# A gated feed-forward stage on one Trainium2 core: one low-rank input in the place of a redundant row, the other added by VectorE

## The chip, the cores and the metric

The kernel runs on one core of a Trainium2 chip. Its engines run side by side, each through its own list of instructions in order: TensorE (PE; PEld is its loading of weights), VectorE (DVE), ScalarE (ACT), GpSimd (POOL) and SyncE (SP), which here does nothing but issue DMAs. A DMA issue that has to wait for data holds up every issue behind it in the same list. Matmul results land in eight banks of PSUM; a bank is free again when the engines that read it are done. The time is the device time of one execution in microseconds (us), the median of several runs.

## The reference

x is 8 x 256 tokens of 512 features. Everything starts from the layer norm xn of x. An attention branch (128 heads with a low-rank latent and rotary parts) gives s, a feed-forward branch gives g, and the result is x + s * silu(g). The change concerns the feed-forward branch only:

```python
def _layernorm(x, axis=-1, eps=1e-05):
    m = jnp.mean(x, axis=axis, keepdims=True)
    v = jnp.var(x, axis=axis, keepdims=True)
    return (x - m) / jnp.sqrt(v + eps)
...
def _qlora_linear(x, wq, A, B):
    w = jnp.tile(wq, (1, 4))
    base = x @ w.T
    lora = x @ A.T @ B.T
    return base + lora * LORA_SCALING
gate = jax.nn.silu(_qlora_linear(x, w1q, a1, b1))
up = _qlora_linear(x, w3q, a3, b3)
return _qlora_linear(gate * up, w2q, a2, b2)
```

Each weight is one quarter (1376 x 128 for w1q and w3q) repeated four times, so the product with the 512 features is a product of the 128 x 1376 quarter with the sum of the four quarters of xn. On top of it comes a term of rank 2. Since xn has mean zero, its 512 features sum to zero, and so do the 128 rows of the quarter sums: any one of these rows is minus the sum of the others.

## The kernel before

The tokens are taken in four blocks (tb = 0 to 3) of 512. `first_phase` (L304) does the feed-forward stage for all four, and in block 3 also slips in the first pieces of the attention stage; it fills about the first 238 us. After it comes a long loop over heads and batches, which the change leaves as it is.

All instructions stand in program order on their engine (`manual_schedule`): what is written earlier is issued earlier. PSUM tiles come from one pool of eight banks (`bank`), SBUF tiles from pools with one (`f1`) or two (`f2`) buffers for each tag; the x tiles (`xt`) have six buffers.

Ahead of the first block: `load_x(0)`, the small weights, `b13_sb` (the second low-rank factors, in 16 loads), `w1_sb`, `w3_sb` and `load_x(1)` are issued on SP, and 48 transposes of an identity (L552) keep TensorE running. Then for a block:

- `norm(tb)` (L370): statistics on VectorE (L376, L377), a reciprocal square root by three steps on small tiles (GpSimd for tb > 0).
- `norm_rest` (L405): the normalized x, on VectorE in block 0 (L412) and on ScalarE after that (L410).
- `turn` (L414): 16 transposes on TensorE; four copies out of PSUM, in turn on ScalarE (L423) and VectorE (L425); then the sum of the four quarters `xs` by two additions on VectorE (L429, L431) and one on GpSimd (L430).
- `narrow` (L443): the 128 rows `mid` = a small weight times xn (bank pm, L446). Rows 32j and 32j+1 (j = 0 to 3) are the low-rank inputs, scaled by 0.5; 16 more in each group of 32 belong to attention's rotary keys and go to DRAM (`krs_d`, L449).
- `down` (L453): another projection for attention (bank pp, L455), written to DRAM (L456); `sum_x` (L144) writes seven pieces of xn, some of them differences taken on GpSimd (L157), to DRAM.
- six units u, each of two chunks of 128 columns of the hidden layer (the last unit has one chunk). `low(tb, u)` (L466) writes the rank-2 term into the banks px and py of the unit's chunks, each by a matmul of 2 rows (L473); the four of a unit lie in four row groups of the array. `main(tb, u)` (L478) adds the products of `w1_sb` and `w3_sb` with `xs` (by `on_columns`, L168: four column groups side by side), takes the SiLU of px on ScalarE (L488) and multiplies it by py on VectorE (L490; L493 and L494 for the three chunks whose rows belong to two quarters). The result is `hT`.
- `fold` (L498) adds the four quarters of `hT` on GpSimd (L508 to L510); `low_out` (L512) computes the low-rank input of the last layer on TensorE (L520) and, after the third quarter, scales and adds it on ScalarE and VectorE (L530, L532).
- `gate_out` (L536): the last layer in four banks (pf), SiLU on ScalarE (L546), and one write of 256 KB for each to DRAM (L547) from `gs`, which has two buffers.

The order between blocks is: `turn(tb+1)`, `low_out(tb, 2)`, `narrow(tb+1)`, `down(tb+1)`, `gate_out(tb)`, then the units of block tb+1. In block 0, `between(0)`, that is `set_up` (L593), stands between `narrow(0)` and `down(0)`: it loads attention weights and a mask on SP (L598 to L601), rearranges them on GpSimd, and reduces the mask on VectorE (L617). In block 3, `between(2)` to `between(7)` follow the units: sums of the rope weights (`sum_w`, GpSimd), `Prepare`, `values`, and four `Project`s (6 us of TensorE each), which also use ScalarE, GpSimd and VectorE. `on_columns` has one line for all its matmuls (L172), so the profile tells them apart by the tile written.

Of the kernel before, what the change touches and what calls it, by code (L numbers as in the profile page):

```python
# [9 lines left out]
F32 = mybir.dt.float32  # L10
# [27 lines left out]
def mla_ffn_gate_kernel(  # L38
# [42 lines left out]
    cs_d = [dram.tile([P, TB], F32, name=f"cs_d{n}") for n in range(NTB)]  # L81
    krs_d = [dram.tile([R, TB], F32, name=f"kr_d{n}") for n in range(NTB)]
# [221 lines left out]
    def first_phase(between):  # L304
# [8 lines left out]
        b13_sb = fw.tile([98, NCH, P], F32, name="b13_sb")  # L313
# [4 lines left out]
        xts, xns, xnT, xsum, mids = {}, {}, {}, {}, {}  # L318
# [8 lines left out]
        def load_chunks(to, of):  # L327

            of = of.rearrange("p (q f) -> p q f", q=4)
            nc.sync.dma_start(  # L330
                out=to[:, 0:8].rearrange("p (q n) m -> p q (n m)", q=4), in_=of[:, :, 0:256]
            )
            nc.sync.dma_start(out=to[:, 8:11, 0:88], in_=of[:, 0:3, 256:344])
            nc.sync.dma_start(
                out=to[:, 8:10, 96:128],
                in_=of[:, 3, 256:320].rearrange("p (m i) -> p m i", m=2),
            )
            nc.sync.dma_start(out=to[:, 10, 96:120], in_=of[:, 3, 320:344])

        for t in (w1_sb, w3_sb, b13_sb):  # L340
            nc.gpsimd.memset(t[:, 8:11, 88:96], 0.0)
            nc.gpsimd.memset(t[:, 10, 120:128], 0.0)
# [18 lines left out]
        for n in range(2):  # L361
            for k in range(2):
                load_chunks(
                    b13_sb[64 * n + 32 * k : 64 * n + 32 * k + 2], b13[32 * k : 32 * k + 2, :]
                )
        load_chunks(w1_sb, w1t)
        load_chunks(w3_sb, w3t)
        load_x(1)

        def norm(tb):  # L370


            mv = f2.tile([P, 4, 2], F32, tag="mv", name=f"mv_{tb}")
            for n in range(4):
                s6 = f2.tile([P, 6], F32, tag="st", name=f"st_{tb}_{n}")
                nc.vector.bn_stats(s6, xts[tb][n])  # L376
                nc.vector.bn_aggr(mv[:, n, :], s6)  # L377
# [21 lines left out]
            off = f2.tile([P, 4], F32, tag="off", name=f"off_{tb}")  # L399
            if tb:  # L400
                nc.gpsimd.tensor_mul(off, mv[:, :, 0], r)
                nc.gpsimd.tensor_scalar(off, off, -1.0, None, ALU.mult)
# [11 lines left out]
        def turn(tb):  # L414
            a = f1.tile([P, KT, TB], F32, tag="act1", name=f"act1_{tb}")
            xnT[tb] = a
            for n in range(4):
                pt = bank(f"xpt_{tb}_{n}")
                for c in range(KT):
                    nc.tensor.transpose(pt[:, ds(c * P, P)], xns[tb][n][:, ds(c * P, P)], ident)  # L420
                pt = pt.rearrange("p (c s) -> p c s", c=KT)
                if n % 2 == 0:
                    nc.scalar.copy(a[:, 0:KT, ds(n * P, P)], pt)  # L423
                else:
                    nc.vector.tensor_copy(a[:, 0:KT, ds(n * P, P)], pt)  # L425

            xs = f2.tile([P, TB], F32, tag="xs", name=f"xs_{tb}")
            xs2 = f1.tile([P, TB], F32, tag="tmp", name=f"xs2_{tb}")
            nc.vector.tensor_add(xs, a[:, 0, :], a[:, 1, :])  # L429
            nc.gpsimd.tensor_add(xs2, a[:, 2, :], a[:, 3, :])  # L430
            nc.vector.tensor_add(xs, xs, xs2)  # L431
            xsum[tb] = xs

        def over_xn(tb, name, weights):
            ps = bank(f"{name}_{tb}")
            for cols in (ds(0, S), ds(S, S)) if name == "pm" and tb == 0 else (ds(0, TB),):
# [6 lines left out]
        def narrow(tb):  # L443
# [3 lines left out]
            mids[tb] = mid  # L447
# [11 lines left out]
        sets, hTs, h4s, mid2ps = {}, {}, {}, {}  # L459
# [6 lines left out]
        def low(tb, u):  # L466

            sets[tb, u] = []
            for i, c in enumerate(pair(u)):
                for k in range(2):  # L470
                    ps = bank(f"p{'xy'[k]}_{tb}_{u}_{i}")
                    r = slice(64 * i + 32 * k, 64 * i + 32 * k + 2)
                    nc.tensor.matmul(  # L473
                        ps, b13_sb[r, c], mids[tb][r], start=True, stop=False, skip_group_check=True
                    )
                    sets[tb, u].append(ps)

        def main(tb, u):  # L478
# [4 lines left out]
            for i, c in enumerate(pair(u)):  # L483
                px, py = sets[tb, u][2 * i : 2 * i + 2]
                on_columns(px, w1_sb[:, c], xsum[tb], False, True)
                on_columns(py, w3_sb[:, c], xsum[tb], False, True)
                gate = f2.tile([P, TB], F32, tag="gate", name=f"gate_{tb}_{u}_{i}")
                nc.scalar.activation(gate, px, AF.Silu)  # L488
                if c < 8:
                    nc.vector.tensor_mul(h[:, c // 2, :], gate, py)  # L490
                else:
# [4 lines left out]
                    )  # L496

# [52 lines left out]
        idle = bank("idle")  # L550
        for n in range(48):
            nc.tensor.transpose(idle[:, ds(n % 4 * P, P)], ident, ident)  # L552
        norm_rest(0, *norm(0))
        turn(0)
        narrow(0)
# [4 lines left out]
        for tb in range(NTB):  # L560
            more = tb + 1 < NTB
            for u in range(6):
                low(tb, u)
# [4 lines left out]
                if u == 1 and more:  # L568
                    stats = norm(tb + 1)
                if u == 4 and more:  # L570
# [9 lines left out]
            if more:  # L580
                turn(tb + 1)
                low_out(tb, 2)
                narrow(tb + 1)
# [3 lines left out]
            gate_out(tb)  # L587

# [388 lines left out]
```

## Time and profile before

| | us |
|---|---|
| median of 3 runs (2010.22 to 2012.34) | 2011.3 |
| the profiled execution, its own time | 2012.79 |
| its span, first to last instruction | 2011.0 |
| feed-forward stage (start to end of the last pf) | 238.5 |
| end of gate_out (pf) in blocks 0, 1, 2, 3 | 71.06, 122.55, 170.77, 238.50 |
| so blocks 1, 2 and 3 take | 51.49, 48.22, 67.73 |
| start of the first unit of block 0 | 21.7 |
| TensorE busy in the whole span | 1998.9 |

A line of the time line reads: start, length, engine, line, operation, tile written <- tiles read, shapes, count; in brackets how long the engine had been idle before it, and what released it. In the chain in order of time the columns are start, length and what. In a table of stretches, each engine has its busy time and its number of instructions, followed by the granted TensorE clock, the DMA share and GB/s. Digits in tile names are left out by the profile (`w1_sb` and `w3_sb` are both `w_sb`, `b13_sb` is `b_sb`). A three-dimensional tile's shape is given as partitions x elements.

### The profile page before, as it was taken

The page shows a single profiled execution, that of the slowest core. Times are in us where ns is not written, and L with a number is a line of the kernel's source. Part 1 is how long each engine was busy: PE and PEld are TensorE (multiplying, and loading weights), DVE is VectorE, ACT ScalarE, POOL GpSimd, SP SyncE. Part 2 cuts the span into 40 slices and gives each one's busy share as a digit, 9 for nine tenths or more (in the row PEclk, how much of TensorE's full clock was granted, in tenths as well). Part 3 has the DMA queues.
Part 4 walks back from the last instruction along what each step waited for, and adds up shares of the span by engine and source line. Part 5 has one row for each costly group of instructions (what it writes and reads, how often), then busy time and mean ns, then how long its engine had stood idle before and what let it go on. Part 6 is the DMA issues. An engine that isn't in the chain of part 4 may idle for free.

```text
span 2011.0 us, 86602 instructions
## 1 busy us (share of the span) xinstructions
PE 1998.9 (99%) x38112; PEld 1412.7 (70%) x38112; DVE 1522.8 (76%) x2601; ACT 1079.4 (54%) x2958; POOL 725.9 (36%) x1076
## 2 busy tenths in 40 slices
PE   9999999999999999999999999999999999999998
PEld 4334577777777777777777767777777767777776
DVE  4332387878788777878787877878787877888788
ACT  2222365565556554555655645565565555556654
POOL 5445545545552323233233233223323323232231
PEclk9999999999999999999999999999999999999999
DMA  5233322222223223222223233222223222222212
GB/s 169 87 113 135 113 95 84 68 87 86 86 82 123 80 91 112 91 87 78 74 86 123 66 112 105 84 81 86 81 92 102 90 93 81 86 86 72 80 55 70
DMA packets 118188, 184.78 MB, mean 92 GB/s; under 512 B 10450, under 2 KB 84082, under 8 KB 117812
## 3 DMA queue, kind: packets, MB, share of 16 engines
q1 hardware_dynamic: 117812, 179.23, 26.4%
q8 instruction: 302, 4.95, 1.0%
q14 instruction: 74, 0.61, 0.1%
HBM read 145.12 MB, written 34.08 MB: 89 GB/s over the span
## 4 chain that ended last, share of the span: by engine, by line
PE 97%; DVE 2%; issue 0%; DMA 0%; ACT 0%; POOL 0%; SPq 0%; DVEq 0%
PE q L172 39%; PE sc L688 34%; PE av L734 11%; PE po L172 2%; PE pf L172 2%; PE px L172 2%; PE py L172 2%; PE px L473 1%; PE pm L172 1%; PE qq L250 1%; PE vps L285 1%; PE pp L172 1%; DVE pt L717 1%; DVE nmx L701 0%; PE pm L520 0%; PE xpt L420 0%
## 5 line engine op out<-in xcount | busy, mean ns | idle before, releaser
L707 ACT ACTIVATE pr<-sc,nmx 128x256 f32<-128x256 f32 x2048 | 816.5, 502 | 473.8 <-DVE nmx L701 471.0
L701 DVE TENSOR_REDUCE nmx<-sc 128x2 f32<-128x512 f32 x1024 | 635.6, 683 | 291.3 <-PE sc L688 267.4
L717 DVE STREAM_TRANSPOSE pt<-pr 128x512 f32<-128x512 f32 x1024 | 635.2, 678 | 0.0
L172 PE MATMUL q<-x,ws 128*32 128x256 f32 x8192 | 488.9, 379 | 0.6 <-POOL ws L136 0.6
L688 PE MATMUL sc<-act,qr 32*128 32x256 f32 x8192 | 489.0, 374 | 0.0
L215 POOL TENSOR_TENSOR e<-e,e 128x256 f32<-128x256 f32 x128 | 93.8, 733 | 1057.5 <-ACT e L210 570.6
L688 PEld LDWEIGHTS sc<-act,qr 32*128 32x128 f32 x8192 | 421.2, 185 | 22.2 <-issue 0.2
L172 PEld LDWEIGHTS q<-x,ws 128*32 128x32 f32 x8192 | 265.7, 110 | 177.2 <-POOL ws L136 1.1
L172 PE MATMUL q<-x,w 128*32 128x256 f32 x6144 | 381.5, 381 | 0.2 <-DMA w<-in_w_rope_dram 0.2
L172 PEld LDWEIGHTS q<-x,w 128*32 128x32 f32 x6144 | 186.9, 110 | 155.0 <-ACT pr L707 35.4
L688 PE MATMUL sc<-kc,qcm 32*128 32x256 f32 x4096 | 281.2, 387 | 0.0
L734 PE MATMUL av<-pt,vpad 128*32 128x128 f32 x8192 | 236.4, 273 | 1.9 <-ACT pr L707 1.2
L734 PEld LDWEIGHTS av<-pt,vpad 128*32 128x32 f32 x8192 | 226.3, 110 | 14.5 <-issue 3.0
L688 PEld LDWEIGHTS sc<-kc,qcm 32*128 32x128 f32 x4096 | 198.4, 184 | 52.1 <-issue 40.1
L210 ACT COPY e<-q 128x256 f32<-128x256 f32 x512 | 204.1, 399 | 27.9 <-PE q L172 26.3
L754 ACT ACTIVATE acc<-av,sides_sb 128x256 f32<-128x256 f32 (+1 forms) x130 | 54.3, 470 | 245.9 <-PE av L734 245.9
L270 POOL TENSOR_TENSOR qcm<-qc,mask_sb 128x1024 f32<-128x1024 f32 x64 | 122.3, 1911 | 9.6 <-ACT qc L260 9.6
L217 POOL TENSOR_TENSOR qr<-e,e 128x256 f32<-128x256 f32 x128 | 93.7, 732 | 10.0
L216 POOL TENSOR_TENSOR e<-e,e 128x256 f32<-128x256 f32 x128 | 93.5, 731 | 10.0
L227 DVE TENSOR_TENSOR qr<-e,q 128x256 f32<-128x256 f32 x128 | 53.9, 421 | 43.4 <-POOL e L215 24.4
L300 POOL COPY vpad<-vall 32x128 f32<-32x128 f32 x256 | 74.9, 293 | 14.8 <-ACT vall L292 4.4
L490 DVE TENSOR_TENSOR hT<-gate,py 128x512 f32<-128x512 f32 x32 | 21.5, 687 | 73.9 <-PE py L172 47.4
(105 smaller groups left out, 1107.4 us busy)
## 6 DMA issues: line engine op xcount, KB each, us to landing
w<-in_w_rope_dram SPq DMA_DIRECT2D x128, 512.0 KB
ws<-sums_d SPq DMA_DIRECT2D x96, 512.0 KB
sums_d<-ws SPq DMA_DIRECT2D x32, 512.0 KB
x<-xs_d SPq DMA_DIRECT2D x28, 256.0 KB
xt<-in_x_dram SPq DMA_DIRECT2D x16, 256.0 KB
xs_d<-xt SPq DMA_DIRECT2D x16, 256.0 KB
gate_d<-gs SPq DMA_DIRECT2D x16, 256.0 KB
g<-gate_d SPq DMA_DIRECT2D x16, 256.0 KB
```

Of the source, the lines that this page charges most:

```text
L172: nc.tensor.matmul(to[tile_], w[:, tile_], x, start=start, stop=stop, skip_group_check=True)
L210: nc.scalar.copy(self.e[i], self.banks[i])
L215: nc.gpsimd.tensor_add(m6, m6, m1)
L216: nc.gpsimd.tensor_add(m7, m7, m6)
L217: nc.gpsimd.tensor_add(self.out(1, 1), self.split(m7), self.split(m5))
L270: nc.gpsimd.tensor_mul(qcm, qks[b, sg // 2][0].rearrange("p (q i) -> p q i", i=32).unsqueeze(2).to_broadcast([P, 8, 4, 32]), mask_sb[:, ds ...
L300: nc.gpsimd.tensor_copy(vpad[rows, :, :, 8 * t + 4 * (sg % 2) :][..., :4], valls[b][rows, :, sg])
L688: nc.tensor.matmul(sc[r][:, h, :], lhs.rearrange("p t i -> p (t i)"), rhs, start=(part == 0 and h == 0), stop=(part == 2), skip_group_chec ...
L701: nc.vector.tensor_reduce(nmx[:, r, :], scs[n, f][r], AX.X, ALU.max, negate=True)
L707: nc.scalar.activation(p[:, h, :], scs[n, f][r][:, h, :], AF.Exp, bias=nmxs[n, f][:, r, h : h + 1])
L717: nc.vector.transpose(pts[n, f // 2, r].rearrange("p k q i -> p q k i")[:, ds(2 * (f % 2), 2)], prs.pop((n, f, r)).rearrange("p h (k j) -> ...
L734: nc.tensor.matmul(av[32 * r : 32 * r + 32, ds(half * P, P)], vpad[:, k, r, :], pt[r][:, k].rearrange("p q i -> p (q i)"), start=(k == 0), ...
```

## The change

Row 0 of the quarter sums is replaced by the first low-rank input, and row 0 of the weights by the first row of the second factor; row 0's own part is carried by subtracting the weights' row 0 from all other rows. So each product of 128 rows brings the first low-rank term with it, and the two-row matmuls of `low` go. There are two such sums now, `xs0` for w1 and `xs1` for w3. The second low-rank term is added by VectorE: its input, spread over all partitions, times a column of factors (`bcol_sb`), plus the bank.

- The weights are prepared once, ahead of block 0: the four rows come by five DMAs on ScalarE's queue; ten matmuls of two rows spread them over all partitions (`firsts`), 28 one-column matmuls turn the second factors into columns (`bcol_sb`), ScalarE copies both, and `less_first` subtracts on GpSimd, for w1 before `turn(0)` and for w3 after it. The 48 identity transposes become 16 and 8, around these. `b13_sb` and its 16 loads go; w1 and w3 come in five loads each.
- `narrow` now also writes the two second inputs from `mid` to DRAM and loads each back to all 128 partitions (`low0`, `low1`), on SP ahead of the `krs_d` writes; ScalarE copies `mid`'s rows 0 and 32 over row 0 of the two sums. Its product is made in two halves of the columns in every block.
- In `main`, VectorE adds the second term to px (into `gate`, of which ScalarE then takes the SiLU in place) and to py (in the bank; or into `hT` for the first chunk of units 0 to 3 in blocks 1 to 3, whose product then goes to GpSimd).
- All four copies of `turn` are on ScalarE in blocks 1 to 3. `narrow(tb+1)` stands ahead of `low_out(tb, 2)`. The norm of block tb+2 is taken after `gate_out(tb)`, that of block 1 still in block 0; `norm_rest` moves from unit 4 to unit 3.

```diff
@@ first_phase, set-up of the weights
-        b13_sb = fw.tile([98, NCH, P], F32, name="b13_sb")
+        bcol_sb = fw.tile([P, 2, NCH], F32, name="bcol_sb")
...
+        rows = f1.tile([P, 3 * TB], F32, tag="h4", name="rows")[:, 0:F]
+        for k, wt in enumerate((w1t, w3t)):
+            nc.scalar.dma_start(out=rows[64 + 32 * k : 65 + 32 * k], in_=b13[32 * k : 32 * k + 1, :])
+            nc.scalar.dma_start(out=rows[65 + 32 * k : 66 + 32 * k], in_=wt[0:1, :])
+        nc.scalar.dma_start(out=rows[0:34], in_=b13)
...
-        for n in range(2):
-            for k in range(2):
-                load_chunks(
-                    b13_sb[64 * n + 32 * k : 64 * n + 32 * k + 2], b13[32 * k : 32 * k + 2, :]
-                )
-        load_chunks(w1_sb, w1t)
-        load_chunks(w3_sb, w3t)
+        for w_sb, wt in ((w1_sb, w1t), (w3_sb, w3t)):
+            load_chunks(nc.sync, w_sb, wt)
@@ turn
-                if n % 2 == 0:
+                if tb or n % 2 == 0:
                     nc.scalar.copy(a[:, 0:KT, ds(n * P, P)], pt)
                 else:
                     nc.vector.tensor_copy(a[:, 0:KT, ds(n * P, P)], pt)
...
-            nc.vector.tensor_add(xs, xs, xs2)
+            nc.vector.tensor_add(xs[0], xs[0], xs2)
+            nc.scalar.copy(xs[1], xs[0])
@@ narrow
-            for cols in (ds(0, S), ds(S, S)) if name == "pm" and tb == 0 else (ds(0, TB),):
+            for cols in (ds(0, S), ds(S, S)) if name == "pm" else (ds(0, TB),):
...
-            mids[tb] = mid
+            nc.sync.dma_start(out=low_d[tb], in_=mid[1:34:32, :])
+            lows[tb] = []
+            for k in range(2):
+                t = f1.tile([P, TB], F32, tag=f"low{k}", name=f"low{k}_{tb}")
+                nc.sync.dma_start(out=t, in_=low_d[tb][k : k + 1, :].to_broadcast([P, TB]))
+                lows[tb].append(t)
+                nc.scalar.copy(xsum[tb][k][0:1], mid[32 * k : 32 * k + 1])
@@ main (low goes)
-        def low(tb, u):
-            sets[tb, u] = []
-            for i, c in enumerate(pair(u)):
-                for k in range(2):
-                    ps = bank(f"p{'xy'[k]}_{tb}_{u}_{i}")
-                    r = slice(64 * i + 32 * k, 64 * i + 32 * k + 2)
-                    nc.tensor.matmul(
-                        ps, b13_sb[r, c], mids[tb][r], start=True, stop=False, skip_group_check=True
-                    )
-                    sets[tb, u].append(ps)
...
-                on_columns(px, w1_sb[:, c], xsum[tb], False, True)
-                on_columns(py, w3_sb[:, c], xsum[tb], False, True)
-                gate = f2.tile([P, TB], F32, tag="gate", name=f"gate_{tb}_{u}_{i}")
-                nc.scalar.activation(gate, px, AF.Silu)
-                if c < 8:
-                    nc.vector.tensor_mul(h[:, c // 2, :], gate, py)
...
+                px, py = (bank(f"p{'xy'[k]}_{tb}_{u}_{i}") for k in range(2))
+                on_columns(px, w1_sb[:, c], xsum[tb][0], True, True)
+                on_columns(py, w3_sb[:, c], xsum[tb][1], True, True)
+                gates.append(f2.tile([P, TB], F32, tag="gate", name=f"gate_{tb}_{u}_{i}"))
+                ups.append((py, h[:, c // 2, :] if tb and i == 0 and c < 8 else py))
+                nc.vector.scalar_tensor_tensor(
+                    gates[i], lows[tb][0], bcol_sb[:, 0, c : c + 1], px, ALU.mult, ALU.add
+                )
+                nc.scalar.activation(gates[i], gates[i], AF.Silu)
+                nc.vector.scalar_tensor_tensor(
+                    ups[i][1], lows[tb][1], bcol_sb[:, 1, c : c + 1], py, ALU.mult, ALU.add
+                )
+            for c, gate, (py, up) in zip(chunks, gates, ups):
+                if c >= 8:
...
+                elif up is py:
+                    nc.vector.tensor_mul(h[:, c // 2, :], gate, py)
+                else:
+                    nc.gpsimd.tensor_mul(up, gate, up)
@@ ahead of block 0
-        idle = bank("idle")
-        for n in range(48):
-            nc.tensor.transpose(idle[:, ds(n % 4 * P, P)], ident, ident)
+        warm(16)
...
+                nc.tensor.matmul(
+                    ps, others[of], two, start=True, stop=True, skip_group_check=True
+                )
+                nc.scalar.copy(one, ps)
...
+                one = rows[r, ds(q * FQ + n * P, CH[n][1])]
+                nc.tensor.matmul(ps[0 : CH[n][1], c : c + 1], one, second, start=True, stop=True)
...
+        warm(8)
+        def less_first(k):
+            w_sb = (w1_sb, w3_sb)[k]
+            nc.gpsimd.memset(w_sb[0:1], 0.0)
+            for one, two in (
+                (w_sb[:, 0:8], firsts[k][:, 0:8]),
+                *((w_sb[:, 8:11][:, a, b], firsts[k][:, 8:11][:, a, b]) for a, b in spots),
+            ):
+                nc.gpsimd.tensor_sub(one, one, two)
         norm_rest(0, *norm(0))
+        less_first(0)
         turn(0)
+        less_first(1)
         narrow(0)
@@ the loop over blocks
-                low(tb, u)
                 main(tb, u)
...
-                if u == 1 and more:
-                    stats = norm(tb + 1)
-                if u == 4 and more:
+                if u == 1 and tb == 0:
+                    stats = norm(1)
+                if u == 3 and more:
                     norm_rest(tb + 1, *stats)
...
                 turn(tb + 1)
+                narrow(tb + 1)
                 low_out(tb, 2)
-                narrow(tb + 1)
                 down(tb + 1)
...
             gate_out(tb)
+            if tb + 2 < NTB:
+                stats = norm(tb + 2)
```

## The prediction

> **What bounds the kernel now.** I read the page first: the busy shares, then the chain that ended last.
>
> ```profile
> PE 1998.9 (99%) x38112; PEld 1412.7 (70%) x38112; DVE 1522.8 (76%) x2601; ACT 1079.4 (54%) x2958; POOL 725.9 (36%) x1076
> ...
> PE 97%; DVE 2%; issue 0%; DMA 0%; ACT 0%; POOL 0%; SPq 0%; DVEq 0%
> ```
>
> TensorE sets the time nearly everywhere. The change touches only the first 238.5 us (the feed-forward stage), so I read that stage by itself: the busy time of PE, PEld, DVE, ACT and POOL in stretches, then granted clock, DMA share and GB/s.
>
> ```profile
> 21.80:60.55 38.75, 38.38 (x325) 12.16 (x328) 16.13 (x30) 13.02 (x20) 30.39 (x64) 1.00 0.42 141
> ...
> 76.00:84.00 8.00, 8.00 (x44) 2.19 (x44) 2.23 (x4) 3.32 (x6) 0.00 (x0) 0.79 0.40 131
> ...
> 122.50:160.30 37.80, 37.68 (x330) 11.93 (x330) 18.75 (x32) 12.23 (x20) 20.38 (x28) 1.00 0.21 70
> ```
>
> Here too TensorE is full while VectorE works less than half of the time; and in one spell of block 1 the clock fell to 0.79. The chain in order of time (start, length) shows what the two-row matmuls cost, here in the first unit of block 3:
>
> ```profile
> 170.77 0.62 PE px L473
> 171.41 0.41 PE px L473
> 171.84 0.99 PE px L172 x8
> 172.83 0.86 PE py L172 x8
> ```
>
> The four low-rank matmuls take 0.62 + 0.41 us, and the product behind them 0.99 instead of 0.86. From their start to the py product it is 2.06 us, of which one product (0.86) is needed: about 1.17 us with the small gaps, in each of 24 units.
>
> The time line of the first block shows what VectorE waits for there:
>
> ```profile
> 1.35 6.90 PE L552 MATMUL idle<-ident 128*128 128x128 f32 x48 [1.35 <-POOL ident masks.py:199]
> ...
> 11.17 3.61 PE L420 MATMUL xpt<-ident,xt 128*128 128x128 f32 x16 [2.92 <-DVE xt L412]
> ...
> 18.44 0.75 DVE L446 TENSOR_SCALAR mid<-pm,cks_sb 128x512 f32<-128x512 f32 x1 [0.27 <-PE pm L172]
> ...
> 21.19 1.74 SPq L449 DMA_DIRECT2D kr_d<-mid  x4
> ...
> 24.03 1.97 SPq L601 DMA_DIRECT2D mask_sb<-in_kmask_dram  x4
> ...
> 29.68 0.16 DVE L617 TENSOR_REDUCE sides_sb<-mask_sb 128x2 f32<-128x8 f32 x1 [10.49 <-DMA mask_sb<-in_kmask_dram]
> 29.79 2.70 DVE L490 TENSOR_TENSOR hT<-gate,py 128x512 f32<-128x512 f32 x4
> ```
>
> VectorE stands still for 10.49 us in front of the reduction of the mask, whose loads are queued on SP behind mid's; only then do its four first products follow. Before, that is hidden: the eight banks let TensorE work two units ahead. Last, the seam from block 0 to block 1:
>
> ```profile
> 53.82 1.68 POOL L508 TENSOR_TENSOR h<-hT 88x512 f32<-88x512 f32 x1
> ...
> 59.39 1.76 DVE L431 TENSOR_TENSOR xs<-xs,xs 128x512 f32<-128x512 f32 x1 [5.05 <-POOL xs L430]
> ...
> 61.18 2.14 DVE L532 SCALAR_TENSOR_TENSOR h<-pm,h 32x512 f32<-32x512 f32 x3
> ...
> 71.50 5.40 SPq L547 DMA_DIRECT2D gate_d<-gs  x3
> ...
> 75.95 1.21 ACT L546 ACTIVATE gs<-pf 128x512 f32<-128x512 f32 x2 [5.95 <-DMA gate_d<-gs]
> ```
>
> ScalarE is held until 75.95 by the write of the first gate tile (there are two such buffers), 4.9 us into block 1.
>
> **What is removed.** 24 units x 1.17 = 28.1 us of TensorE time, 7.0 a block. The 16 loads of b13 leave SP (from 4.16 to 12.4 us), so the weights and x of block 1 are issued 8 us earlier; nothing on the path waited for them.
>
> **What is added in the start.** 20 two-row passes for the weights' first rows: 8 of 512 columns at 0.43 (half of the 0.86 that eight passes in four column groups take), 4 of 264 at 0.22, 8 small ones at 0.1: 5.1 us. 28 one-column products, two passes each, a weight load per pass: no row shows them. From below 0.085 a pass (the warm transposes at 6 to 8 us, 12 in each us), from above 0.144 (6.90 / 48): 4.8 to 8.1; I take 4.8, since they are far narrower on the moving side. They begin when the rows have landed, about 4.0 (ScalarE issues from 0.73, 0.4 each, and the first x tile needed 2.8 from issue to use). With 0.7 for eight transposes TensorE is free at 14.6, not 11.17. The four transposed tiles then take 1.9 instead of 3.6 (3.61 here fell to a clock of 0.50 to 0.59 after 2.9 us of idling; 1.90 in blocks 1 to 3), the last copy 0.7 of which half hides behind the first half of pm, pm 3.6, mid 0.75: **mid is there at 21.0** against 19.19. ScalarE's ten row copies and eight small ones (5.6 us, from 0.20 for one element to 0.59 for 512) keep pace with TensorE; GpSimd's subtractions are costed as 1.3 + 2.5 + 1.25 = 5.1 us for each weight (a 1408-wide memset by 0.956 for 1024; a 1024-wide subtraction at twice 1.28): w1 from 11 to 16, ahead of its half of xs, and w3 from 18.7 to 23.8, just ahead of its first use at 24.5. If that slips, TensorE waits one for one, but VectorE, which is later still, covers it.
>
> **The wait in block 0.** Behind mid, SP now issues a row write (done 1.85 us from its issue: the x tile's 2.81 less 0.99 for its 256 KB at 264 GB/s; bounds 0.35, an issue alone, and 4.45, the landing of a gate tile), waits for it, issues two broadcasts (0.8 us), and only then the four kr_d writes and what follows. From the first kr_d issue to the mask reduction took 29.68 - 21.19 = 8.5 us. So VectorE starts at 21.0 + 0.1 + 1.85 + 0.8 + 8.5 = **32.25**; its broadcasts landed before. Queued behind the reduction are all the additions that free TensorE's banks.
>
> **VectorE's work.** Per chunk two three-operand additions. Their kind on a bank is shown only as L532: 2.14 / 3 = 0.71; bounds 0.675 (2.70 / 4) and 0.751 (L446, with a per-partition scalar); writing back into a bank isn't shown. I take 0.70: 22 x 0.70 = 15.4. Products: 14 x 0.675 = 9.45 in block 0, 10 in later blocks (four go to GpSimd at about 1.3): 6.75. The norm, 4 x 0.80 + 0.6 = 3.8, stands inside block 0 and behind gate_out later, where VectorE is free. Block 0 needs 28.65, so its last product ends at **D0 = 32.25 + 28.7 = 60.95**; TensorE alone would be there by about 44.
>
> **From D to the end of the block.** Only after the last SiLU (D - 1.4) does ScalarE copy the transposed tiles (0.57 each, now all four on it): pm from D - 0.2 to D + 3.4, the low-rank output 0.86, pp 3.43, pf 10.30: D + 18.0. Block 0 ends at 78.95, against 71.06: **+7.9**.
>
> **Blocks 1 and 2.** TensorE alone would need 48.22 - 7.0 = 41.2. VectorE by itself: D + 18.0 + 1.1 + 22.15 = D + 41.3. But ScalarE is held by the gate tiles. GpSimd's fold (4.27) and its addition (1.27), VectorE's addition 1.76 and mid 0.75: mid at D + 8.2. From mid to the landing of the first gate tile was 75.95 - 64.10 = 11.85, and 2.65 comes in front for the row write and the broadcasts: D + 22.7. Two gate tiles (1.21) and two SiLUs (1.2) later VectorE may multiply, with 19.4 us still to do: next D = D + **44.5**. Block 1 falls from 51.49 (3.3 of it the slow-clock spell) to 44.5: **-7.0**; block 2 from 48.22: **-3.7**.
>
> **Block 3.** 67.73 by the chain, less 7.0. The first unit's product on GpSimd now stands ahead of the two sums of rope weights (5.8 us), the spread (1.9) and the placing (1.3), and the second unit's behind them, so low_out of quarter 0 waits some 1.6 us: 62.3, **-5.4**. VectorE's lag is covered by the projections (6.04 each).
>
> Sum: 7.9 - 7.0 - 3.7 - 5.4 = -8.2. Each seam leaves TensorE idle for up to 3.4 us ahead of pm. In this trace 2.9 us of idling (8.25 to 11.17) led to a clock of 0.50 until 14.5; half a clock over that length costs 1.7. In the earlier seams the D chain absorbs it, in the last it counts: **-6.5**. (The Trainium skill, "TensorE: Matmul & The Clock Gate", section "The HAM clock gate", puts the fall behind a whole idle window of about 3.4 us: by that alone the last seam might stay just under it and the sum be -8.2; the row at 76 to 84, where waits of a few tenths among thin matmuls sufficed, and the 2.9 us here speak for the shorter idling.) The rest, 1773 us, is untouched. The sum is on the profiled execution (span 2011.0, its own time 2012.79, 1.5 above the median); taken off the median, 2011.3 - 6.5 = **2004.8**.
>
> **Rivals.** (a) *TensorE stays the bound*: VectorE keeps within the lead of eight banks. For it: VectorE works only 16 of 38.75 us there. Against: 28.65 us of work behind a start at 32. It would give 2011.3 - 28.1 - 3.3 = 1980; half of it, with mask and gate tiles landing 4 us earlier, 1992. Chance 0.12 for below 1998.
> (b) *It does nothing measurable*: the start costs more. With passes at 0.144 (+3.3) and a cold clock for the first rows (+2.5) D0 and all behind it move 5.8: 2010.6. For it: the clock was 0.50 after idling; against: the small products themselves keep TensorE busy. Chance 0.24.
> (c) *Slower*: VectorE's additions are stretched while GpSimd works. L431 takes 0.692 alone and 1.754 beside it. With 66 additions in blocks 0 to 2 on the bound, the gain is gone at 0.80 each; with a mixture of 60% of 0.69 and 40% of 1.754, 1.12 each, it is 66 x 0.42 = 27.7 more: 2032. Against: L490, which like them has one operand in a bank, keeps 0.687 beside a busy GpSimd, and L431 has none in a bank. Chance 0.14 for all that is slower.
>
> **How the numbers follow.** The forecast has 0.50. 0.2% (4 us) is what a measurement of this kernel can tell from no change: faster 0.50 + 0.12 = 0.62, same 0.24, slower 0.14. Additions at 0.751 add 66 x 0.05 = 3.4, the row write at 4.45 another 2.6 a block (7.8); at 0.35 it takes 1.5 a block off; the clock takes 1.7 off. Range 1995 to 2013.5, leaving about 0.08 below and 0.11 above.
>
> **What would show it.** mid of block 0 at 21, the mask reduction at 32, and additions at 0.70 in groups behind it; TensorE waiting on VectorE through block 0; pf ending near 79, 123.5, 168 and 232 (before 71.06, 122.55, 170.77, 238.50). A block 0 that ends by 70 would make (a) right; additions over 0.8, (c); a transposition starting after 18, (b).

## The result, and the profile after

The changed kernel takes 2019.87 us (median of 6 runs, 2016.53 to 2021.43) against 2011.15 us before (2010.22 to 2012.34): ratio 1.0041, interval 1.0028 to 1.0053. It is slower, where 2004.8 was forecast. The profiled execution has a span of 2017.7 us and its own time of 2019.45, against 2011.0 and 2012.79.

The page of the profile after, busy time of each engine and then the chain that ended last:

```profile
PE 1993.3 (99%) x38084; PEld 1422.9 (71%) x38084; DVE 1574.0 (78%) x2671; ACT 1093.9 (54%) x2994; POOL 750.6 (37%) x1103
...
PE 93%; DVE 3%; DMA 1%; issue 1%; SPq 1%; POOL 1%; ACT 0%; POOLq 0%; ACTq 0%; DVEq 0%
```

TensorE is busy for 5.6 us less than before (1998.9) and the kernel is still longer: 4% of the chain has gone over to other engines, DMAs and queues. Where, the ends of the four last stages (pf) of the feed-forward blocks tell, in us from the span's start; the predicted row is worked out from the prediction's terms:

| pf ends | block 0 | block 1 | block 2 | block 3 | rest of the span |
|---|---|---|---|---|---|
| before | 71.06 | 122.55 | 170.77 | 238.50 | 1772.5 |
| predicted (block) | 78.95 | +44.5 | +44.5 | +62.3 | untouched |
| after | 95.16 | 137.83 | 183.22 | 243.84 | 1773.9 |
| after, block by block | +24.1 | -8.8 | -2.8 | -7.1 | +1.4 |

Blocks 1 to 3 win 18.7 us, close to the 16.1 forecast for them; block 0 loses 24.1 instead of 7.9. TensorE's time line of the first 32 us (start, duration, what, and in brackets its idle time before and what ended it; rows of one kind are put together, and the shape printed is that of the last of them):

```profile
1.35 3.67 PE L587 MATMUL idle<-ident 128*128 128x128 f32 x16 [1.35 <-POOL ident masks.py:199]
4.95 4.66 PE L604 MATMUL first<-rows,others 2*128 2x512 f32 x6
10.08 0.69 PE L604 MATMUL first<-rows,others 2*128 2x64 f32 x2 [0.47 <-ACT first L607]
11.07 4.73 PE L604 MATMUL first<-rows,others 2*128 2x24 f32 x8 [0.30 <-ACT first L607]
...
17.50 3.63 PE L616 MATMUL bcol<-ident,rows 2*128 2x1 f32 x17
...
27.47 1.97 PE L587 MATMUL idle<-ident 128*128 128x128 f32 x8
29.23 2.71 PE L445 MATMUL xpt<-ident,xt 128*128 128x128 f32 x16
```

The profile counts each of these matmuls twice (ten give 20 rows); one such half is called a pass. Six of the two-row passes, four of 512 and two of 264 columns by the order of the code, take 4.66 us; at the 0.43 and 0.22 that were assumed it would be 2.2. The one-column products run from 17.5 to 27.5, and the first transposition of block 0 starts at 29.23; before it was 11.17. VectorE's and SP's time lines show that what comes behind follows at about the forecast distance:

```profile
35.67 0.75 DVE L472 TENSOR_SCALAR mid<-pm,cks_sb 128x512 f32<-128x512 f32 x1 [0.33 <-PE pm L173]
46.83 0.16 DVE L708 TENSOR_REDUCE sides_sb<-mask_sb 128x2 f32<-128x8 f32 x1 [10.41 <-DMA mask_sb<-in_kmask_dram]
46.91 0.74 DVE L513 SCALAR_TENSOR_TENSOR gate<-low,bcol_sb,px 128x512 f32<-128x512 f32 x1
47.56 0.75 DVE L517 SCALAR_TENSOR_TENSOR py<-low,bcol_sb,py 128x512 f32<-128x512 f32 x1
```

```profile
36.45 0.62 SPq L474 DMA_DIRECT2D low_d<-mid  x1
38.16 0.81 SPq L478 DMA_DIRECT2D low<-low_d  x2
```

From the first transposition to mid's end (36.42) it is 7.2 us (forecast 6.4; the terms that the prediction names for it add up to 6.6), from there to the mask reduction 10.4 (11.25), the row write is done 1.7 us after its issue (1.85), and the additions are 0.74 to 0.75 long but start 0.66 apart (0.70).

### The profile page after: what moved, and what is told of

Its sections match the earlier page's. It is cut to its first block, busy times and chain, and to the rows that moved or that the text cites. A ratio compares the mean times of both kernels' runs of the same rounds, so it can differ in the third digit from the quotient of the medians.

```text
span 2017.7 us, 86730 instructions
## 1 busy us (share of the span) xinstructions
PE 1993.3 (99%) x38084; PEld 1422.9 (71%) x38084; DVE 1574.0 (78%) x2671; ACT 1093.9 (54%) x2994; POOL 750.6 (37%) x1103
## 4 chain that ended last, share of the span: by engine, by line
PE 93%; DVE 3%; DMA 1%; issue 1%; SPq 1%; POOL 1%; ACT 0%; POOLq 0%; ACTq 0%; DVEq 0%
PE q L173 39%; PE sc L779 33%; PE av L825 11%; PE po L173 2%; PE pf L173 2%; PE pm L173 1%; PE px L173 1%; PE py L173 1%; PE vps L286 1%; PE qq L251 1%; DVE pt L808 1%; PE first L604 1%; PE pp L173 1%; DMA wo_sb<-in_w_o_dram 0%; DVE nmx L792 0%
## 5 line engine op out<-in xcount | busy, mean ns | idle before, releaser
L228 DVE TENSOR_TENSOR qr<-e,q 128x256 f32<-128x256 f32 x128 | 53.9, 421 | 40.8 <-POOL e L216 24.1
L301 POOL COPY vpad<-vall 32x128 f32<-32x128 f32 x256 | 74.9, 293 | 10.7 <-PE av L825 2.7
L851 POOL TENSOR_TENSOR acc<-acc,acc 128x256 f32<-128x256 f32 (+1 forms) x66 | 48.5, 755 | 39.1 <-ACT acc L845 39.1
```

The costliest lines, as they stand in the source:

```text
L301: nc.gpsimd.tensor_copy(vpad[rows, :, :, 8 * t + 4 * (sg % 2) :][..., :4], valls[b][rows, :, sg])
```

## The experiments

Theory P: TensorE's preparation ahead of block 0, at half clock and with waits for ScalarE, is the whole loss. "Half clock" stands for instructions of a kind that take twice the time that they take elsewhere in these traces. All times are compared with runs of the kernel before on the same chip, whose median was 2010.6 to 2011.5.

**e3: the kernel before, with the preparation alone.** Loads, passes, products and copies are those of the change; what they produce is used by nothing, and everything else stays.

```diff
-        idle = bank("idle")
-        for n in range(48):
-            nc.tensor.transpose(idle[:, ds(n % 4 * P, P)], ident, ident)
+        warm(16)
+        firsts = []
...
+                nc.scalar.copy(bcol_sb[p_, k, c_], ps[p_, c_])
+        warm(8)
```

> The kernel of before with the preparation alone added: the five loads of rows on ScalarE's queue, 16 transposes, ten two-row matmuls, 28 one-column products, their copies, eight transposes; the results are not used. Theory P: before is bound by TensorE, so the later first transposition (29 instead of 11.2) shows nearly in full: 2025 to 2029. The prediction's cost (TensorE free at 14.6) would give 2013 to 2015. If loads hide it, 2011.

Measured: 2025.03, ratio 1.0067 (1.005 to 1.0084), 14.1 us more.

```profile
29.61 2.52 PE L441 MATMUL xpt<-ident,xt 128*128 128x128 f32 x16
...
76.96 10.51 PE L172 MATMUL pf<-w_sb,h 128*32 128x512 f32 x96
```

The first transposition starts at 29.61, close to after's 29.23, and pf ends at 87.47 in block 0 instead of 71.06. The preparation by itself costs more than the change's whole loss.

**e1: the 28 products and their copies moved behind `narrow(0)`,** where TensorE waits for nothing that it could do sooner.

```diff
-        for k in range(2):
-            ps = bank(f"bcol{k}")
...
         narrow(0)
+        columns()
         between(0)
```

> The changed kernel with the 28 one-column products (and their copies) moved from ahead of turn(0) to behind narrow(0); nothing is left out. Theory P: TensorE's preparation ahead of the first transposition delays block 0 one for one. The products filled 17.3 to 27.5, so the first transposition starts near 19 instead of 29.2, mid is there near 26.5 (36.4), the mask reduction runs near 37 (46.8), gate_out of block 0 ends near 85 (95.2), and the time is near 2010 (2019.9). Theory M: the mask's loads and the queues set VectorE's start whatever TensorE did before; then the reduction stays near 47, gate_out of block 0 near 95, and the time near 2020.

Measured: 2012.24 (2007.21 to 2014.9), ratio to before 1.0003 (0.9994 to 1.0012), 7.6 us less than after. TensorE's time line:

```profile
4.96 2.60 PE L604 MATMUL first<-rows,others 2*128 2x512 f32 x6
8.31 0.43 PE L604 MATMUL first<-rows,others 2*128 2x64 f32 x2 [0.76 <-ACT first L607]
9.05 4.73 PE L604 MATMUL first<-rows,others 2*128 2x24 f32 x8 [0.30 <-ACT first L607]
...
17.54 2.63 PE L445 MATMUL xpt<-ident,xt 128*128 128x128 f32 x16
20.17 3.66 PE L173 MATMUL pm<-act,ck_sb 128*32 128x256 f32 x64
23.76 2.10 PE L617 MATMUL bcol<-ident,rows 2*128 2x1 f32 x18
```

The transposition comes 11.7 us earlier: 10.0 by the products, the rest because in this execution the first passes met the full clock (2.60 for what took 4.66) and lost it 4 us later. It was the fastest of the ten executions, 5.0 us below their median; in e7, whose preparation is the same, the first passes took 4.66 again and the transposition starts at 19.56. Behind pm, 18 passes of the products take 2.10 us instead of 3.86 in after. The loss against before is gone, but no gain is left either.

**e4: 48 idle transpositions ahead of the passes instead of 16** (`warm(48)`), to begin them at full clock.

> The changed kernel with 48 identity transposes ahead of the preparation instead of 16. In the changed kernel a pass of 512 columns took 0.85 and not 0.43: half a clock. If the clock only had not risen yet, the passes now run at 0.43 and the one-column passes near 0.1, the preparation lasts some 12 instead of 24 us from 8.3 on, the first transposition starts at 21 to 23, and the time is near 2012 to 2014. If thin matmuls themselves let the clock fall again after some 3.4 us, only the first passes take 0.43, the rest 0.85, the first transposition starts at 29 to 32, and the time is 2020 to 2023. If the passes cost 0.85 at any clock, all of them do from the start: start near 33, time near 2024.

Measured: 2017.85, ratio 1.0035 (1.0022 to 1.0048):

```profile
8.13 2.42 PE L604 MATMUL first<-rows,others 2*128 2x512 f32 x6
11.07 0.69 PE L604 MATMUL first<-rows,others 2*128 2x64 f32 x2 [0.51 <-ACT first L607]
12.06 4.73 PE L604 MATMUL first<-rows,others 2*128 2x24 f32 x8 [0.30 <-ACT first L607]
```

The first six take 2.42 us, the 512-column passes at 0.40 to 0.43; the eight behind them 4.73 as in after. The granted clock of this profile says the same: 1.00 from 8.13 to 10.60, 0.50 from 12.06 to 17.00. So the clock doesn't only start low: it falls again within 3 us while TensorE is given nothing but such passes, with pauses of at most 0.51. The first transposition comes at 30.23, as expected for a clock that falls again; the time lies 2 us below the range given for it.

**e8: the same with all 128 rows contracted,** 126 of them zeros.

```diff
+        nc.vector.memset(rows, 0.0)
-                    ps, others[of], two, start=True, stop=True, skip_group_check=True
+                    ps, others[:, k], two, start=True, stop=True, skip_group_check=True
...
-            r = slice(32 * k, 32 * k + 2)
+            r = slice(0, P)
```

> As e4 (48 idle transpositions first), but the 20 passes and the 28 products contract all 128 rows, 126 of them zeros, instead of 2. If the clock falls because few rows of the array are in use: the 20 passes stay at 0.40 to 0.43 each for 512 columns, end near 15 instead of 18.5 and the one-column products cost 6 us instead of 10: first transposition of block 0 at 20 to 23 (e4 30.2), time 2010 to 2014. If it falls because of the pauses between them (0.3 to 0.5 us for ScalarE's copies) or of the zeros: as e4, 0.85 from about 11 us on and 2017 to 2020.

Measured: 2027.13, ratio 1.0079 (1.0064 to 1.0094). The total missed the expectation, since the passes start only at 17.93. By the code a pass over all rows waits for all five loads of `rows`, the last of them issued only at 9.95; the profile doesn't name what ended this wait. The durations answer the question all the same:

```profile
17.93 4.27 PE L606 MATMUL first<-rows,others 128*128 128x512 f32 x6 [9.54 <-issue]
22.67 0.44 PE L606 MATMUL first<-rows,others 128*128 128x64 f32 x2 [0.47 <-ACT first L609]
23.41 2.65 PE L606 MATMUL first<-rows,others 128*128 128x24 f32 x8 [0.30 <-ACT first L609]
...
27.55 2.96 PE L618 MATMUL bcol<-ident,rows 128*128 128x1 f32 x18
...
31.77 3.86 PE L618 MATMUL bcol<-ident,rows 128*128 128x1 f32 x18
```

After 9.5 us of standing still the first six run slowly, but these passes bring the clock up, and it stays up through the same pauses of 0.3 to 0.5 us: 2.65 for the eight that took 4.73 in e4, with the same order, columns and waits (granted clock 1.00 from 23.41 to 26.06). With two rows these eight take 4.73 in the profiles of after, e1, e2, e3, e4 and e7 alike. Rows in use, not pauses, make the difference (one execution with 128 rows). The one-column products let it fall in spite of their 128 rows: 2.96 for the first 18 passes, 3.86 for the second 18, as in after.

**e2 and e7: the mask reduction (L708) moved into block 3,** alone and together with e1.

```diff
-        nc.vector.tensor_reduce(
-            sides_sb, mask_sb.rearrange("p (n e) -> p e n", e=2), AX.X, ALU.add
-        )
...
         elif step == 2:
+            nc.vector.tensor_reduce(
+                sides_sb, mask_sb.rearrange("p (n e) -> p e n", e=2), AX.X, ALU.add
+            )
```

> The changed kernel with only the mask's reduction moved on VectorE from set_up to block 3; nothing is left out. The reduction stood in front of the first addition until 46.8. If VectorE is the bound of block 0 (the prediction's step), the first addition starts when the first broadcast has landed, 41 to 42, gate_out of block 0 ends near 90 (95.2) and the time is near 2015. If TensorE is the bound of block 0, nothing changes: 2020.

> The two moves of e1 and e2 together, the 20 two-row passes left where they are. Theory P: they add up, -7.6 of e1 and -2.8 of e2 from after's 2019.9, so 2008.5 to 2011; first addition at 31 to 33. If both win the same stretch of VectorE's wait, no more than e1: 2012.

Measured: e2 2017.03, ratio 1.0031 (1.002 to 1.0042); e7 2011.51, 1.0003 (0.9994 to 1.0012), no more than e1. In e2 the first addition comes at 42.19 instead of 46.91, but pf of block 0 starts only 2.0 us earlier (82.70 against 84.69). One of the two longest waits from 62 to 76 us is:

```profile
ACT xt L435 <- POOL off L427: 3.3, 1, 3.3
```

ScalarE's normalization of block 1 waits for GpSimd's small steps. The first addition itself now waits for px, in e2 and in e7 (40.49), where px stands behind the columns and pp. The mask is a real wait, but two others stand right behind it; that GpSimd's steps took the rest of the gain is read from the trace and wasn't tried by itself.

**e5 and e6: the preparation replaced by loads.** The first factors come to all 128 partitions by broadcast loads, the second as 22 rows turned by one transposition; e6 has the mask late too.

```diff
+            for one, two in by_chunks(firsts[k], wt[0:1, :].to_broadcast([P, F])):
+                nc.scalar.dma_start(out=one, in_=two)
```

> The first factors reach all 128 partitions as broadcast loads, the second factors as 22 rows turned by one transposition; the 20 two-row passes and 28 one-column products are gone, and 48 idle transpositions stand first as in the kernel before. Theory P (the preparation on TensorE is the whole loss): first transposition of block 0 at 11 to 14 us (after 29.2), mid of block 0 at 20 to 23, first addition of VectorE at 31 to 35 (46.9), last stage of block 0 starts at 64 to 70 (84.6 or so in after) and the time is 2002 to 2007. Rival D (the loads are no better: 1.4 MB more written to SBUF in the first 15 us delay x, the quarter sums' weights or the subtraction): first transposition still at 11 to 14, but the first addition after 40 and the time 2009 to 2015. Rival S (GpSimd's or VectorE's new work is the loss, TensorE's preparation only hides it): first addition above 40 with the loads landed before 15 us.

> The run before with the mask's reduction moved into block 3. Theory P: first addition another 3 to 5 us earlier, at 27 to 31, but e2 gave back more than half of such a gain to a wait of ScalarE for GpSimd; so the last stage of block 0 starts 1.5 to 4.5 earlier than in the run before, and the time is 2000 to 2005. If less_first's subtractions on GpSimd now end last ahead of the first addition, nothing is gained: as the run before.

Measured: 2019.53, ratio 1.004 (1.0025 to 1.0055), and 2018.46, 1.0028 (1.0018 to 1.0038). None of the three accounts had the cause: 34 issues stand on ScalarE's queue, and ScalarE makes its first copy for block 0 at 29.58, though the first transposition starts at 17.47.

```profile
15.05 3.09 ACTq L374 DMA_DIRECT2D first<-in_w1t_dram  x5
18.23 4.32 ACTq L376 DMA_DIRECT2D brow<-in_b_dram  x5
22.59 2.49 ACTq L374 DMA_DIRECT2D first<-in_w3t_dram  x5
25.17 3.01 ACTq L376 DMA_DIRECT2D brow<-in_b_dram  x5
...
29.58 1.08 ACT L463 COPY act<-xpt 128x512 f32<-128x512 f32 x2
```

The loss has only moved: in this trace an issue takes 0.25 to 1.1 us of its engine's list, like an instruction (the expectation of e9 below counts 28 of them). The mask gains nothing where ScalarE is the last.

**e9 and e10: one broadcast load for each weight, on SP behind the weight's own loads;** columns late as in e1, 48 idle transpositions first, no two-row pass. e10 has the mask late as well.

```diff
+            nc.sync.dma_start(out=to, in_=wt[0:1, :].to_broadcast([P, F]))
```

> Second way of taking the preparation off TensorE's head, after e5's 28 loads on ScalarE's queue held up ScalarE until 28 us: the first factors come as one broadcast load each on SP's queue, behind the weights that they are taken from; the column products stand behind narrow(0) as in e1; 48 idle transpositions first, as in before. No two-row pass is left. Theory P: first transposition of block 0 at 11 to 13 us, mid at 18 to 21, mask reduction at 29 to 33 (e1 35.3), last stage of block 0 starts at 67 to 71.5 (e1 73.2), time 2006 to 2010.5. If the 1.4 MB of broadcasts hold up the weights or x (rival D): first addition at 35 or later, time 2012 or more.

> As the run before, with the mask reduction in block 3. Theory P: the first addition comes when the low rows, w1 and the columns are there, 25 to 30 us; the last stage of block 0 starts 2 to 4 us earlier than in the run before; time 2003 to 2008. If, as in e7, the late block 0 isn't bound by VectorE's start, it gains nothing: 2006 to 2011.

Measured: 2008.67, ratio 0.9992 (0.9983 to 1.0001), and 2009.55, 0.9994 (0.9985 to 1.0004). The first transposition still waits, until 14.64 in e9 (x's last statistics end at 11.6, in after at 7.5): the load of b13's 34 rows is issued at 0.72 here, beside those of x, and at 6.74 in after. Mid waits still longer. VectorE in e9:

```profile
23.14 2.96 DVE L452 TENSOR_TENSOR xs<-xs,xs 128x512 f32<-128x512 f32 x1 [3.13 <-POOL xs L451]
26.03 0.74 DVE L468 TENSOR_SCALAR mid<-pm,cks_sb 128x512 f32<-128x512 f32 x1
```

In e10 the mask is late and the first addition comes at 36.12, waiting for px; nothing is won by it. pm is done at 22.4 in e9, but mid stands on VectorE behind an addition that waits for GpSimd, which does the first weight's subtraction first.

**e13: both taken away.** Only the four needed rows of b13 are loaded; GpSimd's addition comes before the subtractions; VectorE does the second subtraction and ScalarE its row. These are tried together, not one by one.

```diff
-        nc.scalar.dma_start(out=rows[0:34], in_=b13)
+        for k in range(2):
+            nc.scalar.dma_start(out=rows[32 * k : 32 * k + 2], in_=b13[32 * k : 32 * k + 2, :])
...
-        less_first(0)
         turn(0)
-        less_first(1)
         narrow(0)
+        less_first(0)
+        less_first(1)
         columns()
```

> As e9, but nothing stands ahead of the first transposition: only the four needed rows of b13 are loaded, GpSimd's part of the sum of x comes before the subtractions, VectorE takes the second weight's subtraction and ScalarE its row. If the prediction's steps behind the head hold: first transposition at 11 to 12 us, mid written at 19 to 20.5, mask reduction at 29.5 to 31.5, last stage of block 0 starts at 67 to 69.5, time 2001 to 2005. If the loss reappears (the subtractions end too late, TensorE waits for w1 or w3): first addition after 33, time 2007 or more.

Measured: **2000.01** (1999.61 to 2002.1), ratio 0.9945 (0.993 to 0.996). TensorE, then VectorE:

```profile
10.67 2.03 PE L442 MATMUL xpt<-ident,xt 128*128 128x128 f32 x16 [1.27 <-DVE xt L434]
12.73 3.66 PE L173 MATMUL pm<-act,ck_sb 128*32 128x256 f32 x64
16.32 2.10 PE L596 MATMUL bcol<-ident,rows 2*128 2x1 f32 x18
...
23.38 5.50 PE L173 MATMUL pp<-act,wdn_sb 128*32 128x512 f32 x32
```

```profile
17.08 0.74 DVE L469 TENSOR_SCALAR mid<-pm,cks_sb 128x512 f32<-128x512 f32 x1
...
28.55 0.16 DVE L690 TENSOR_REDUCE sides_sb<-mask_sb 128x2 f32<-128x8 f32 x1 [7.42 <-DMA mask_sb<-in_kmask_dram]
29.91 0.75 DVE L510 SCALAR_TENSOR_TENSOR gate<-low,bcol_sb,px 128x512 f32<-128x512 f32 x1 [1.20 <-PE px L173]
```

x's first statistics start at 3.98 (7.19 in e9). Mid ends at 17.82, the reduction follows 10.7 later, and pf ends at 77.46, 120.10, 163.20 and 223.83. With the transposition at its old place, 3.9 us ahead of the forecast 14.6, the change is 11.5 us faster than before where 6.5 was forecast: what the rest of the prediction gives for such a start, within about 1 us.

**e11, e12 and e15: gate tiles and the seams.** e11 is e10 with three gate tiles instead of two (`bufs=3`), e12 is e10 with `warm(24)` between `turn(tb + 1)` and `narrow(tb + 1)`, e15 has both.

> As the run before with three instead of two gate tiles, so that VectorE's addition of a unit waits less for GpSimd's product of the unit before. If that wait (4.6 us in all in after) is on the path: 1 to 3 us less than the run before. If other waits take its place: the same within 1.

> As e10 with 24 idle transpositions between a block's turn and its mid product at each of the three seams, so that TensorE doesn't stand still there. If standing still is what lets the clock fall (pm 5.3 instead of 3.66 at a seam): all three pm at 3.7 and 1 to 3 us less. If the transpositions only push the mid product back: 1 to 3 us more.

> e11 with the 24 idle transpositions at each seam of e12. In e12 they took 2.3 off e10; if independent of the gate tiles: 2002 to 2005. If e11 already won the same stretch: 2004.5 to 2007.

Measured: e11 2005.79, ratio 0.9976 (0.9967 to 0.9985); e12 2007.22, 0.9983 (0.9974 to 0.9993); e15 2006.14, 0.9974 (0.9963 to 0.9985). The product pm at the seams of e10, and the last one of e11:

```profile
66.90 5.35 PE L173 MATMUL pm<-act,ck_sb 128*32 128x256 f32 x64 [3.17 <-ACT act L444]
111.26 3.66 PE L173 MATMUL pm<-act,ck_sb 128*32 128x256 f32 x64 [1.92 <-ACT act L444]
...
155.22 5.35 PE L173 MATMUL pm<-act,ck_sb 128*32 128x256 f32 x64 [3.18 <-ACT act L444]
```

```profile
152.92 3.66 PE L173 MATMUL pm<-act,ck_sb 128*32 128x256 f32 x64 [1.60 <-ACT act L444]
```

At e10's first and last seam TensorE stands idle for 3.17 and 3.18 us and pm takes 5.35. In e10's block 2 an addition of VectorE waits for GpSimd's product:

```profile
147.25 0.75 DVE L509 SCALAR_TENSOR_TENSOR gate<-low,bcol_sb,px 128x512 f32<-128x512 f32 x1 [1.01 <-POOL hT L526]
```

With the third gate tile this wait goes away, ScalarE's copies come sooner, the idling falls to 1.60 and pm keeps its 3.66. In e12 all three take 3.66, since the transpositions fill the gap. They don't add up: where the gap is short, the transpositions only push pm back (blocks 1 and 2 take 42.35 us each in e11, 43.30 in e15). e11 gained more than was expected of it (3.8 against 1 to 3), e12 what was expected (2.3).

**e14 and e16: all together.** e14 is e13 with the mask late, three gate tiles and the idle transpositions at the seams; e16 also puts the columns behind block 0's pp.

> e13 with the mask reduction in block 3, three gate tiles and 24 idle transpositions at each seam. If these are independent: first addition at 24 to 28, last stage of block 0 starts at 63 to 67, all three later mid products at 3.7, time 1996 to 2002. If the early start is eaten by ScalarE's wait for GpSimd (as in e2): within 1.5 of e13.

> As e14, with the 28 one-column products behind block 0's pp products instead of ahead of them. If the products' low clock is what held up e14's first addition (33.5 us): pp takes 3.6 to 3.7, first addition at 28 to 31, last stage of block 0 starts at 64 to 67.5, time 1995 to 1998. If the columns then take their slow 8 us all the same, only behind pp, and the first px starts no earlier than 32: as e14, 1998 to 2000.

Measured: 1998.76, ratio 0.9934 (0.9918 to 0.9951), and **1998.24**, 0.9935 (0.9921 to 0.9948). Both beat the two kernels, but not e13 by a measurable amount: the slow clock behind the one-column products meets whatever comes next. In e14 that is pp (6.42 us instead of 3.6):

```profile
26.09 6.42 PE L173 MATMUL pp<-act,wdn_sb 128*32 128x512 f32 x32
```

In e16 it is the first px and py (1.94 and 1.93 instead of 1.03):

```profile
15.83 3.64 PE L173 MATMUL pp<-act,wdn_sb 128*32 128x512 f32 x32
...
27.37 1.94 PE L173 MATMUL px<-xs,w_sb 128*32 128x512 f32 x8
29.08 1.93 PE L173 MATMUL py<-xs,w_sb 128*32 128x512 f32 x8
```

## Why the prediction was wrong

**The failing step is "TensorE is free at 14.6"**: it was free at 29.23. Its terms, against the trace of after:

| term | forecast | measured | off by |
|---|---|---|---|
| start of the passes | 4.0 | 4.95 | 0.95 |
| 20 two-row passes | 5.1 | 12.55, 1.5 of it waiting for ScalarE | 7.45 |
| 28 one-column products | 4.8 | 9.97 | 5.17 |
| eight transpositions | 0.7 | 1.76 | 1.06 |

That is 14.6 us; the miss of the whole was 15.1 by the medians (2019.87 less 2004.8) and 13.2 between the two profiled executions. Three assumptions failed. The full clock: at full clock the passes take 6.3 (2.42 for the first six in e4; 0.44, 2.65, 0.43 and 0.40 for the others in e8) and the products 5.9 (twice the 2.94 that the first 14 took in e13), so the clock is some 9.8 of the 14.6 (an estimate from these figures; the eight transpositions are in it with 1.06). The prices: 6.3 and 5.9 are themselves 2.3 more than the 5.1 and 4.8 of the forecast, which priced the narrow passes too low. And the copies were to "keep pace with TensorE": several parts share a bank, and a pass into it starts only when ScalarE has read the part before, which stops TensorE four times, 1.5 in all.

**The step "the small products themselves keep TensorE busy"**, with which rival (b) was held down, is what misled: TensorE was busy, and the clock fell all the same (e4). Rival (b) named place and cause, a cold clock and passes at 0.144 at the start, and its sign, a transposition after 18, came (29.23); but it was priced at 5.8, and it was 14.6. The Trainium skill ("TensorE: Matmul & The Clock Gate", section "The HAM clock gate") says that the clock follows how busy the array has been and that some 3.4 us of matmuls, however many, bring it to full speed. By that the passes would have been at full speed from about 8.4 us on (an estimate, 4.95 + 3.4); here they were not by 17.5, and e8 shows that the rows in use count. The measurement decides.

**Right, within 1 to 2 us, behind that step**: mid to reduction 10.4 (11.25), VectorE's work in block 0 28.8 (28.65), D to the end of block 0 19.5 (18.0, and 1.7 for the slow clock that was counted at the last seam only), and from D to D (VectorE's last product of a block, at 75.68, 120.01 and 163.71) 44.3 in block 1 and 43.7 in block 2 (44.5 each). By the ends of pf, block 1 takes 42.67, block 2 45.39, with the slow clock of the last seam, and block 3 60.62 (62.3). e13 tests the rest of the sum: with the transposition at 10.67 its blocks 1 to 3 take 42.64, 43.10 and 60.63, and the kernel 2000.0.

**Partly by luck, the 44.5 of blocks 1 and 2.** ScalarE got on with the third gate tile at D + 20.6 and D + 20.1 (96.27 and 140.10), not D + 22.7; in block 1 that held its first SiLU up by only 0.65, and VectorE's first addition had waited 5.53 for TensorE's px. From VectorE's first product on it took 20.4 and 20.7 instead of 19.4, in block 2 with 1.2 of waiting for GpSimd's products. Two errors of 1 to 2 us nearly cancel. TensorE, for which the prediction allows 41.2, stood still for only 1.92 us in all of block 1 (2.95 in block 2), so it was close to being the bound itself.

**Rival (a)**, TensorE as the bound: its half was 1992, and the lowest median of any variant is e16's 1998.24; in after TensorE's chain gave 4% to others, where it would have had to take more. **Rival (c)**, stretched additions: 0.74 to 0.76 each in all of after's stage, GpSimd busy or not, so what it rested on didn't reach these additions. Slower it was, for another reason.

**Not foreseen**: the wait of an addition for GpSimd's product through the two gate tiles (e11), and 1.4 us more in the rest of the span. The latter wasn't tried by itself.

## What to carry to other kernels

Price a preparation by the rows and columns that it puts to work, not by TensorE being busy: here long runs of matmuls of two rows or of one moving column let the clock fall to half and left it so for what followed, so put them where something else is the bound. Ask of each one-time step what stands first behind it on each engine's queue; here e5 moved the delay from TensorE to ScalarE's issues, e9 to a load ahead of x and to GpSimd, and only e13 took it away. And when a wait is taken away and half of the gain comes, look for the wait right behind it before giving up the idea.

## What the runs showed of the hardware

- The clock fell during matmuls of two rows with no pause over 0.51 us (e4: 2.42 us for six, then 4.73 for eight that take 2.65 in e8 with 128 rows; granted clock 0.50 and 1.00) and of one moving column (e13: 18 passes in 2.10 us, 18 more in 2.88, and pp behind them 5.50 instead of 3.6).
- The granted clock that the profile records doesn't always show it: in after the stretch from 0 to 28 us reads 1.00, though its passes take twice 0.43 and the first 16 transpositions 0.23 each; in e13 it reads 0.74 for 18 to 23 us. The lines, for after and e13, end in the granted clock, the DMA share and GB/s.

```profile
0.00:28.00 28.00, 25.11 (x95) 18.56 (x96) 7.29 (x24) 5.91 (x19) 8.97 (x36) 1.00 0.47 131
```

```profile
18.00:23.00 5.00, 5.00 (x40) 4.85 (x40) 3.13 (x5) 3.27 (x11) 4.78 (x10) 0.74 0.49 141
```

- How long TensorE may stand still: in the profiles of this case every wait of 2.85 us or more ahead of the transpositions or of pm was followed by 3.6 to 3.7 for the 16 transpositions instead of 2.0, or by 4.9 to 6.0 for pm instead of 3.66. Yet no single length divides the two. Ahead of pm, 2.76 (e9) and all waits up to 2.35 kept the full clock, but in e2 2.14 us ahead of the last four transpositions lost it (1.04 for the four; 0.63 after 2.13 in e6). Ahead of py, 3.12 kept it in e11 (granted 1.00 from 47 to 61), while in after 2.09 was followed by a px of 1.93 instead of 1.07.

```profile
51.71 1.07 PE L173 MATMUL py<-xs,w_sb 128*32 128x512 f32 x8 [3.12 <-DVE gate L509]
```
